# Layer 2's centring pass by 16 rows x 32 columns of all channels, with a second buffer for its stores

## The chip, the cores and the metric

The kernel runs on one core of a Trainium2 chip. The metric is device time in microseconds, from one launch to its end; the time before is the median of three runs. Durations, waits and packets come from one further execution that the hardware profiler recorded. The core's engines are PE (matrix multiply), DVE (vector), ACT (scalar, activations), POOL (GpSimd) and SP, which in this kernel issues every DMA; 16 DMA engines move the data.

## The reference

The input is 16 images of 64 x 64 tokens with 256 channels, fp32. Four layers follow one another, each `x = x + layer(group_norm(x))`:

```
x = x + _L0_conv_ref(_gn(x), ...)   # linear attention with a layer norm
x = x + _L1_conv_ref(_gn(x), ...)   # channel and spatial gates, a scan, batch norm
x = x + _L2_conv_ref(_gn(x), ...)   # 3x3 involution: kernels made from each token
x = x + _L3_conv_ref(_gn(x), ...)   # 7x7 involution, the same with 49 taps
```

What matters here is the input of the last layer. With `_gn` in 32 groups,

```
def _gn(v, G=32, eps=1e-5):
    g = v.reshape(B_, H_, W_, G, C_ // G)
    m = jnp.mean(g, axis=(1, 2, 4), keepdims=True)
    s = jnp.var(g, axis=(1, 2, 4), keepdims=True)
    return ((g - m) / jnp.sqrt(s + eps)).reshape(v.shape)
```

layer 3 needs each image minus its groups' means ("centred"), with a border of zeros, in 7 x 7 neighbourhoods: `out[h,w,c] = sum over 49 taps of kgen[h,w,group,tap] * centred[h+i-3, w+j-3, c]`. The division by the standard deviation is done elsewhere.

## The kernel before, in words

All instructions are unrolled; the kernel has three stages that follow one another. Stage a is layer 0 with the first statistics of layer 1, then comes a short stage for the scan and the statistics of layer 1 (until about 3,880 us), stage b does the end of layer 1 and all of layer 2, stage c is layer 3. Images pass between them through DRAM tensors: `x3_d` holds the output of layer 2, token after token with 256 channels (1 KB) each; `c3_d` holds the same with channels first; `strips` holds the centred image as layer 3 reads it: `strips[image, quarter, row, w, tile, 64]`. A quarter is 64 channels. A row is cut into NTC = 8 tiles of TC = 8 columns, and each tile is kept with three more columns on either side (w = 0 to 13), so a column near a tile's edge is stored twice. There are nine more rows and the outer columns that hold zeros. Stage c loads 128 consecutive (row, w) entries of it as 128 partitions of 2 KB.

Stage b (L912 to L1282) runs under a manual schedule, that is, instructions are issued in the order in which they are written. It runs 151 turns; in turn n, four lagged jobs each take one of eight parts (`rc`) of an image: `end_of_layer1` (lag 0: DVE multiplies, L989, ACT applies the gate, L995, POOL adds the input, L999; x2 is stored), `projected` (lag 12, PE, L1052), layer 2's involution (lag 20: PE transposes shifted rows, ACT copies them, L1102, DVE multiplies with the token's kernels, L1121, POOL sums the first half over nine taps, L1136 and L1137, DVE reduces the second half, L1271, and adds the residual, L1274), and `centred` (lag 30: the centring pass, for all images but the last). Statistics of the image that ended are made by `norm2` and `norm3` in between; `norm3` leaves the 256 means of an image on every partition (`gmb`).

The DMAs of a turn are all issued on SP's queue, in this order: loads for the next turn (x2p, x2r, x1 in two, pf in two), stores of what the turn before made (x2; x3 in two; c3 in two; 16 strip stores), and the load of the next turn's xc in two. A DMA takes one of eight completion semaphores in turn, and SP issues it only when the DMA before it on that semaphore has landed, so at most eight are under way.

The centring pass before: part `rc` of an image is one quarter of the channels in half of the rows. `centred_from` gives two sources in `x3_d`; `load_centred` (or the loop of stage c) loads them into `xc`, of 128 partitions x 16 rows x 64 channels: partition 64 g + w holds column w of 16 rows of image half g, and every run is 64 channels, 256 B. `centred_strips` subtracts the means in place (L892, POOL) and returns 16 stores: for either half g and each of eight tiles the 14 columns of the tile with its borders (11 at the image's edge) x 16 rows x 256 B. A tile `xc` has two buffers in stage b.

Stage c (L1286 to L1545) has 16 x 4 x 11 = 704 turns: one for each image, quarter and pair of tile rows. A turn loads patches for four turns ahead (`xw`, 6 buffers, L1414) and residuals (`rx`, L1434), runs 32 small matmuls against them (`involution7`, L1446), lets ACT, DVE and POOL combine two rows (L1456, L1457, L1464), makes part of the next quarter's matrices (`matrices`, L1380 to L1395), and stores. The centring of the last image is spread over this stage: at every 44th turn of the first eight images (n % 44 == 1) xc is loaded into one of the xw buffers (L1520), a turn later POOL subtracts, and of the 16 stores up to four are issued a turn (L1522).

`maps` and `fac` are small per-token maps of layer 1 (6.6 KB a partition) in the pool `gates`, which stays open until stage b ends.

Of the kernel before, what the change touches and what calls it, by code (L numbers as in the profile page):

```python
# [9 lines left out]
F32 = mybir.dt.float32  # L10
# [5 lines left out]
P = 128  # L16
C = 256
HW = 64
# [3 lines left out]
NB = 32  # L22
# [6 lines left out]
TR, TC = 3, 8  # L29
NTR, NTC = 22, HW // TC  # L30
# [6 lines left out]
def network(ctx: ExitStack, tc: tile.TileContext, a: dict, out: bass.AP):  # L37
    nc = tc.nc
    NI = a["x"].shape[0]
# [5 lines left out]
    def const(name, shape, src=None):  # L45
        t = cp.tile(shape, F32, tag=name, name=name)
        if src is not None:
            nc.sync.dma_start(out=t, in_=src)
        return t
# [5 lines left out]
    def gconst(name, shape):  # L55
        return gp.tile(shape, F32, tag=name, name=name)

    ident = const("ident", [P, P], a["ident"])
    gmat = gconst("gmat", [P, P])
    nc.sync.dma_start(out=gmat, in_=a["gmat"])  # L60
# [1 line left out]
    nc.vector.memset(mhalf, -0.5)  # L62

    ab = gconst("ab", [P, 2, NI, 2])
    fac = gconst("fac", [P, NI, NB])

    ngm1 = gconst("ngm1", [P, NI, 2])
    mean1 = gconst("mean1", [P, NI, 2])


    maps = gconst("maps", [P, 2, NI, NB + 4])
    nc.vector.memset(maps, 0.0)

    gm3 = const("gm3", [P, NI, 2])
# [7 lines left out]
    x3_d = dram.tile([NI, NT, C], F32, tag="x3_d", name="x3_d")  # L82
    c3_d = dram.tile([NI, P, 2, NT], F32, tag="c3_d", name="c3_d")
    strips = dram.tile([NI, 4, HW + 9, TC + 6, NTC, 64], F32, tag="strips", name="strips")
# [92 lines left out]
    with ExitStack() as st:  # L177
# [12 lines left out]
        for v in (wo[:, 0], wo[:, 1], bout):  # L190
            mean = small.tile([P, 1], F32, tag="wmean", name="wmean")
# [13 lines left out]
        wk = st.enter_context(tc.tile_pool(name="a_work", bufs=2))  # L205
# [5 lines left out]
        loaded, stores = {}, []  # L211

        def load(kind, i, ch):

            tag = {"xin": "xin", "xn": "xn"}.get(kind, "x1")
            t = wk.tile([P, 2, CT], F32, tag=tag, name=kind, bufs=4 if tag == "x1" else 2)
            src = a["x"][i, ch]
            if kind == "xm":
                src = x1_d[i, :, :, ch * CT : (ch + 1) * CT].rearrange("h p t -> p h t")
            nc.sync.dma_start(out=t, in_=src)  # L220
            loaded[kind, i, ch] = t
# [355 lines left out]
        for n in range(LAST + 16):  # L577
            m, t = divmod(n, NCH)
# [64 lines left out]
    with ExitStack() as st:  # L643
        pc = st.enter_context(tc.tile_pool(name="s_const", bufs=1))
        wk = st.enter_context(tc.tile_pool(name="s_work", bufs=3))
# [22 lines left out]
        with tc.tile_pool(name="s_conv", bufs=1) as pcv:  # L668
# [4 lines left out]
                out=lsa.rearrange("p i j c -> p (i j c)"), in_=a["lsa_w"].partition_broadcast(P)  # L673
# [27 lines left out]
        for n in range(10):  # L701
            delta, c = n // 2, n % 2
# [28 lines left out]
        with tc.manual_schedule():  # L731
            steps = [(ch, g) for ch in range(NCH) for g in range(NG)]
            rows, ins, hsts = {}, {}, {}
# [23 lines left out]
            for n, (ch, g) in enumerate(steps):  # L757
# [18 lines left out]
                b, k = g * 8, min(8, NI - g * 8)  # L776
# [8 lines left out]
        n = NI * NCH  # L785
# [61 lines left out]
            ALU.mult,  # L847
        )

    def folded(pool, name, mean, var, gamma, beta, shift):  # L850


        v = pool.tile([P, 5], F32, tag=f"{name}_v", name="v")
        for n, src in enumerate((mean, var, gamma, beta, shift)):
            if src is None:
                nc.vector.memset(v[:, n : n + 1], 0.0)
            else:
                for k in range(2):
                    nc.sync.dma_start(out=v[k * 64 : k * 64 + 64, n : n + 1], in_=a[src])
        sb = pool.tile([P, 3], F32, tag=f"{name}_sb", name="sb")  # L860
        nc.vector.tensor_scalar(v[:, 1:2], v[:, 1:2], BN_EPS, None, ALU.add)
        nc.gpsimd.tensor_tensor(v[:, 1:2], v[:, 1:2], mhalf[:, 0:1], ALU.pow)
        nc.vector.tensor_tensor(sb[:, 0:1], v[:, 1:2], v[:, 2:3], ALU.mult)
        nc.vector.tensor_tensor(v[:, 0:1], v[:, 4:5], v[:, 0:1], ALU.subtract)
        nc.vector.tensor_tensor(v[:, 0:1], v[:, 0:1], sb[:, 0:1], ALU.mult)
        nc.vector.tensor_tensor(sb[:, 1:2], v[:, 0:1], v[:, 3:4], ALU.add)
        nc.vector.tensor_scalar(sb[:, 2:3], sb[:, 0:1], -1.0, None, ALU.mult)
        return sb
# [11 lines left out]

    def centred_from(i, rc):

        quarter, q = divmod(rc, 2)
        x3n = x3_d[i].rearrange("(g r w) c -> g w r c", g=2, w=HW)
        return [
            x3n[g][:, q * 16 : q * 16 + 16, quarter * 64 : quarter * 64 + 64] for g in range(2)
        ]

    def centred_strips(i, rc, xc, mean):

        quarter, q = divmod(rc, 2)
        nc.gpsimd.tensor_tensor(  # L892
            xc, xc,
            mean[:, quarter * 64 : quarter * 64 + 64].unsqueeze(1).broadcast_to([P, 16, 64]),
            ALU.subtract,
        )
        parts = []
        for g in range(2):
            r0 = 3 + 32 * g + 16 * q
            for tj in range(NTC):  # L900
                lo, hi = max(0, tj * TC - 3), min(HW, tj * TC + TC + 3)
                c0 = lo - tj * TC + 3
                parts.append((
                    strips[i, quarter, r0 : r0 + 16, c0 : c0 + hi - lo, tj, :].rearrange(
                        "r w c -> w r c"
                    ),
                    xc[g * HW + lo : g * HW + hi],
                ))
        return parts


    with ExitStack() as st:  # L912
# [7 lines left out]
        gmb = {}  # L920
# [28 lines left out]
        loaded, stores, begun = [], [], []  # L949
# [8 lines left out]
        def taken(name):  # L958

            n = [k for k, _ in loaded].index(name)  # L960
            return loaded.pop(n)[1]
# [9 lines left out]
            ))  # L971

        def load_centred(i, rc):
            load("xc", [P, 16, 64], *(
                (lambda t, g=g: t[g * HW : (g + 1) * HW], src)
                for g, src in enumerate(centred_from(i, rc))
            ))

        def end_of_layer1(i, rc):
# [206 lines left out]
            )  # L1186

        def centred(i, rc):
            stores.extend(centred_strips(i, rc, taken("xc"), gmb[i]))

# [93 lines left out]
    with ExitStack() as st:  # L1286
# [201 lines left out]
        for n, (i, quarter, t) in enumerate(turns):  # L1488
            if quarter == t == 0:

                pm = sm.tile([P, CT], F32, tag="sm", name="pm")
                for k in range(2):
                    for j in range(2):
                        nc.tensor.matmul(
                            pm[64 * k : 64 * k + 64, 2 * j : 2 * j + 2],
                            lhsT=ident[:, 64 * j : 64 * j + 64], rhs=rs3[:, i, :],
                            start=True, stop=True,
                        )
                msk = small.tile([P, 2, 2, 2], F32, tag="msk", name="msk")
                nc.vector.tensor_tensor(  # L1500
                    msk.rearrange("p j k g -> p (j k) g"),
                    pm[:, 0:4].unsqueeze(2).broadcast_to([P, 4, 2]),
                    gpar.unsqueeze(1).broadcast_to([P, 4, 2]),
                    ALU.mult,
                )
            if t == 0:
                making = iter(())
                if n + NTT < len(turns):
                    making = matrices(*turns[n + NTT][:2])
            if n + 4 < len(turns):  # L1510
                pats.append(load_patches(*turns[n + 4]))
            if t % 2 == 0:
                ex = wk.tile([P, 2, TR * HW], F32, tag="ex", name="ex", bufs=4)
                rx = res.pop(0)
            if n + 2 < len(turns) and turns[n + 2][2] % 2 == 0:
                res.append(load_residual(*turns[n + 2]))
            if n % gap == 1 and n // gap < NCH:
                xc = wk.tile([P, 16, 64], F32, tag="xw", name="xc", bufs=6)
                for g, src in enumerate(centred_from(NI - 1, n // gap)):
                    nc.sync.dma_start(out=xc[g * HW : (g + 1) * HW], in_=src)  # L1520
            for dst, src in strip_stores[:4]:
                nc.sync.dma_start(out=dst, in_=src)  # L1522
            del strip_stores[:4]
            if done and done[0][0] == n:
                for dst, src in done.pop(0)[1]:
                    nc.sync.dma_start(out=dst, in_=src)  # L1526
            if n + 2 in features:
                cs[features[n + 2]] = load_reduced(*features[n + 2])
            involution7(i, quarter, t, wms[i, quarter], msk, pats.pop(0), ex[:, t % 2], rx[:, t % 2])
            if n % gap == 2 and n // gap < NCH:  # L1530
                strip_stores.extend(centred_strips(NI - 1, n // gap, xc, mean))
            for _ in range(STEPS[t]):
                next(making, None)
            if n in features:
                tp, k = features[n]
                reduced(k, tp, cs.pop((tp, k)))
            if t == NTT - 1:
                next(making, None)
                del wms[i, quarter]
            if t % 2 or t == NTT - 1:  # L1540
                parts = halves(ex, out[i, quarter * 64 : quarter * 64 + 64], t - t % 2)
                done.append((n + 3, [(d, s) for s, d in parts]))
# [111 lines left out]
```

## Time and profile before

| | us |
|---|---|
| Median of three runs | 8,946.06 |
| The runs | 8,943.62 to 8,962.98 |
| The profiled execution | 8,976.86 |
| Its span, first to last instruction | 8,974.9 |

Busy time in that span: PE 7,219.9 us (80%), weight loads 5,328.9 (59%), DVE 6,420.8 (72%), ACT 4,992.0 (56%), POOL 2,764.1 (31%); the DMA queue that SP feeds kept the 16 engines busy 62.5% of the time, with 1,616,994 packets of 1,682 MB. These shares are averages over stages of different kinds, so they don't say what sets the time in any of them; the tables by stretch do.

What the centring pass does in the profile: POOL's subtract L892 takes 2.36 us (120 times in stage b, 8 times in stage c at 2.38 us). There are 256 loads of xc, 256 KB each, and 2,048 strip stores, 1,536 of 56 KB and 512 of 44 KB. In stage b they run from 4,046 to 6,571 us, in stage c from 6,632 to 7,728 us.

Of the views: in a list of waits, "A <- B: total, times, longest" says that the engine of A stood idle before line A until B came. In a timeline a row has the start in us, the length, engine, line and operation, what is written from what, and how many were merged. A DMA row on SP is its issue, not its transfer.

### The profile page before, as it was taken

How to read it: one execution, taken by the hardware profiler on the slowest of the kernel's cores; microseconds unless marked ns; L12 is line 12 of the kernel's file. 1: busy time of each engine (PE TensorE's matmuls, PEld its weight loads, DVE VectorE, ACT ScalarE, POOL GpSimd, SP SyncE). 2: the span in 40 equal slices, each digit the busy share in tenths (PEclk: the TensorE clock that was granted, in tenths of full speed). 3: DMA queues.
4: the chain of work that ended last, by engine and by line, in shares of the span. 5: the costliest groups of instructions: out<-in, count | busy, mean ns of one | idle time of the engine just before them, and what ended most of it. 6: DMA issues, size and time to landing. Idle time of an engine off the chain costs nothing. (4 is left out here: it accounts for less than half of the span.)

```text
span 8974.9 us, 210876 instructions
## 1 busy us (share of the span) xinstructions
PE 7219.9 (80%) x84764; PEld 5328.9 (59%) x84764; DVE 6420.8 (72%) x8639; ACT 4992.0 (56%) x11904; POOL 2764.1 (31%) x1962
## 2 busy tenths in 40 slices
PE   7998988888899977477777777777758888888887
PEld 4666666666666653145554445545547666677776
DVE  6676666776666665679989988999946565566665
ACT  3555555555555554666655556565545555566655
POOL 0111111111111110157766666676712121111112
PEclk9999999999999987789888888888879999999999
DMA  6533333333333333867878878887768888888887
GB/s 219 167 121 122 122 124 123 125 118 125 127 106 104 106 113 118 250 201 219 222 215 226 223 217 223 227 224 211 182 193 240 248 249 244 247 256 255 255 256 233
DMA packets 1617971, 1695.46 MB, mean 189 GB/s; under 512 B 855265, under 2 KB 1221170, under 8 KB 1615842
## 3 DMA queue, kind: packets, MB, share of 16 engines
q1 hardware_dynamic: 1616994, 1681.98, 62.5%
q8 instruction: 668, 10.94, 0.5%
q14 instruction: 309, 2.53, 0.1%
HBM read 1234.54 MB, written 469.76 MB: 190 GB/s over the span
## 5 line engine op out<-in xcount | busy, mean ns | idle before, releaser
L279 PE MATMUL pq<-wq,xn 128*128 128x384 f32 x4096 | 1476.1, 504 | 105.4 <-DVE va L295 55.3
L1121 DVE TENSOR_TENSOR pd<-xs,pw 128x1152 f32<-128x1152 f32 x1024 | 1305.6, 1349 | 13.3 <-ACT xs L1102 13.3
L1380 PE MATMUL pk<-rt,span 64*128 64x176 f32 x12288 | 1217.4, 334 | 108.5 <-issue 58.5
L1395 DVE TENSOR_TENSOR wm<-pk,spanb 128x704 f32<-128x704 f32 x896 | 1174.2, 1354 | 171.6 <-PE pk L1380 157.7
L1390 ACT ACTIVATE wm<-pk,spanb 128x176 f32<-128x176 f32 x2560 | 989.8, 543 | 542.0 <-PE pk L1380 519.5
L1380 PEld LDWEIGHTS pk<-rt,span 64*128 64x128 f32 x12288 | 997.5, 195 | 212.5 <-issue 82.9
L1136 POOL TENSOR_TENSOR pd<-pd 128x2048 f32<-128x2048 f32 (+2 forms) x384 | 1064.6, 2772 | 180.9 <-DVE pd L1121 160.8
L279 PEld LDWEIGHTS pq<-wq,xn 128*128 128x128 f32 x4096 | 763.7, 195 | 572.7 <-DVE va L295 88.5
L1464 POOL TENSOR_TENSOR ex<-ex,rx 128x192 f32<-128x192 f32 (+2 forms) x768 | 436.8, 570 | 1888.1 <-DVE ex L1457 1401.0
L1446 PE MATMUL pa<-wm,xw 126*32 126x48 f32 x45056 | 694.4, 211 | 260.9 <-issue 245.8
L1457 DVE SCALAR_TENSOR_TENSOR ex<-pa,msk,ex 128x192 f32<-128x192 f32 x704 | 292.3, 415 | 752.2 <-ACT ex L1456 718.6
L1446 PEld LDWEIGHTS pa<-wm,xw 126*32 126x32 f32 x45056 | 574.4, 112 | 426.9 <-issue 376.2
L1098 PEld LDWEIGHTS pt<-ident,pad 128*128 128x128 f32 x4608 | 535.7, 150 | 239.6 <-issue 104.4
L1073 PE MATMUL pr<-x2r,wrs 128*64 128x512 f32 x512 | 364.5, 853 | 374.3 <-DMA x2r<-x_d 368.5
L1102 ACT COPY xs<-pt 128x512 f32<-128x512 f32 x1152 | 591.6, 602 | 121.1 <-PE pt L1098 115.5
L448 POOL TENSOR_TENSOR rsy<-ss,mhalf 128x4 f32<-128x4 f32 x128 | 129.8, 1014 | 1709.4 <-DVE ss L446 1709.4
L1098 PE MATMUL pt<-ident,pad 128*128 128x128 f32 x4608 | 615.7, 290 | 48.4 <-ACT rt L1076 29.3
L1271 DVE TENSOR_REDUCE x<-pd 128x512 f32<-128x4608 f32 x128 | 633.7, 4951 | 1.9
L1052 PE MATMUL px<-x2p,wis 128*128 128x512 f32 x1024 | 531.7, 664 | 111.4 <-ACT c L1150 68.2
L436 PE MATMUL py<-wo,oT 128*128 128x256 f32 x2048 | 472.8, 383 | 28.6 <-DVE va L295 28.6
L1456 ACT ACTIVATE ex<-pa,msk 128x192 f32<-128x192 f32 x704 | 298.3, 424 | 347.1 <-PE pa L1446 211.5
L445 ACT ACTIVATE sq<-y 128x256 f32<-128x256 f32 x512 | 213.0, 416 | 422.6 <-DVE y L441 414.6
(238 smaller groups left out, 12722.0 us busy)
## 6 DMA issues: line engine op xcount, KB each, us to landing
xw<-strips SPq DMA_DIRECT2D x1408, 256.0 KB
xn<-in_x SPq DMA_DIRECT2D x256, 512.0 KB
x_d<-x SPq DMA_DIRECT2D x256, 512.0 KB
strips<-xc SPq DMA_DIRECT2D x1536, 56.0 KB
xin<-in_x SPq DMA_DIRECT2D x128, 512.0 KB
x<-in_x SPq DMA_DIRECT2D x128, 512.0 KB
xm<-x_d SPq DMA_DIRECT2D x128, 512.0 KB
x<-x_d SPq DMA_DIRECT2D x128, 512.0 KB
```

What stands on the lines that cost most here:

```text
L279: nc.tensor.matmul(pq[:, dd, 0:384], lhsT=xn[:, h, tok], rhs=wq[:, h, hf * 384 : (hf + 1) * 384], start=(h == 0), stop=(h == 1),)
L436: nc.tensor.matmul(py[:, q, :], lhsT=oT[hf][:, q * P : (q + 1) * P], rhs=wo[:, hf, :], start=(hf == 0), stop=(hf == 1),)
L1052: nc.tensor.matmul(px, lhsT=w[:, h, fh * P : (fh + 1) * P], rhs=x2[:, h], start=(h == 0), stop=(h == 1),)
L1098: nc.tensor.transpose(pt[:, k, h * P : (h + 1) * P], lines[:, h, rc * 4 + e + k, 2 * j : 2 * j + P], ident,)
L1102: nc.scalar.copy(xs[:, e : e + 2, j, :], pt)
L1121: nc.vector.tensor_tensor(pd[:, r].rearrange("p (g f) k -> p g f k", f=16), run[:, oh * 9 * P : (oh + 1) * 9 * P].rearrange("p (g f k) -> ...
L1136: nc.gpsimd.tensor_tensor(pd[..., 0:n], pd[..., 0:n], pd[..., n : 2 * n], ALU.add)
L1271: nc.vector.tensor_reduce(x3[:, :, P:C], pd1, AX.X, ALU.add)
L1380: nc.tensor.matmul(pkv[:, b, m], lhsT=span[half, first + gg, s0 : s0 + P], rhs=rto[half, o // 4 * 2 + m, :], start=True, stop=True,)
L1390: nc.scalar.activation(dst[:, m // 2, m % 2], pkv[:, m // 2, m % 2], AF.Identity, bias=spanb[:, g0 + m : g0 + m + 1],)
L1395: nc.vector.tensor_tensor(dst, pkv, spanb[:, g0 : g0 + 4].rearrange("p (b m) -> p b m", b=2).unsqueeze(3).broadcast_to([P, 2, 2, NTL]), AL ...
L1446: nc.tensor.matmul(pav[p0 : p0 + 32, :, tj * TC : (tj + 1) * TC], lhsT=xw[0:TILE_IN, k, tj, 32 * q : 32 * q + 32], rhs=wm[q][0:TILE_IN, (t ...
```

## The change

A part of the image is now 16 rows x 32 columns of all 256 channels: `part` gives the rows, `th` the left or right half of the eight tiles. A partition holds tokens that lie 8 columns apart: partition 16 u + r has, for row r and column u within a tile, the four tiles of that half. The load is four DMAs, one a tile, in runs of 1 KB (256 channels). POOL subtracts the means from `xc` into a second tile, `cen`, in which the quarter comes before the tile, so that the four tiles of a quarter are 1 KB in a row, as they are in `strips`. The stores are twelve: for each quarter the 8 columns themselves, the last three columns as the right neighbours' left border, and the first three as the left neighbours' right border. In stage b `cen` has two buffers of its own; in stage c it takes another of the six buffers of `xw`. `maps` and `fac` move into a pool that is closed ahead of stage b.

```diff
+    maps_st = ExitStack()
+    mp = maps_st.enter_context(tc.tile_pool(name="maps", bufs=1))
...
-    fac = gconst("fac", [P, NI, NB])
+    fac = mp.tile([P, NI, NB], F32, tag="fac", name="fac")
...
-    maps = gconst("maps", [P, 2, NI, NB + 4])
+    maps = mp.tile([P, 2, NI, NB + 4], F32, tag="maps", name="maps")
...
+    maps_st.close()
...
     def centred_from(i, rc):
-        quarter, q = divmod(rc, 2)
-        x3n = x3_d[i].rearrange("(g r w) c -> g w r c", g=2, w=HW)
-        return [
-            x3n[g][:, q * 16 : q * 16 + 16, quarter * 64 : quarter * 64 + 64] for g in range(2)
-        ]
+        part, th = divmod(rc, 2)
+        x3n = x3_d[i].rearrange("(r t u) c -> u r t c", t=NTC, u=TC)
+        return [x3n[:, part * 16 : part * 16 + 16, th * 4 + t, :] for t in range(4)]

-    def centred_strips(i, rc, xc, mean):
-        quarter, q = divmod(rc, 2)
+    def centred_strips(i, rc, xc, cen, mean):
+        part, th = divmod(rc, 2)
         nc.gpsimd.tensor_tensor(
-            xc, xc,
-            mean[:, quarter * 64 : quarter * 64 + 64].unsqueeze(1).broadcast_to([P, 16, 64]),
+            cen.rearrange("p q t c -> p t q c"),
+            xc.rearrange("p t (q c) -> p t q c", q=4),
+            mean.rearrange("p (q c) -> p q c", q=4).unsqueeze(1).broadcast_to([P, 4, 4, 64]),
             ALU.subtract,
         )
         parts = []
-        for g in range(2):
-            r0 = 3 + 32 * g + 16 * q
-            for tj in range(NTC):
-                lo, hi = max(0, tj * TC - 3), min(HW, tj * TC + TC + 3)
-                c0 = lo - tj * TC + 3
+        rows = slice(3 + 16 * part, 19 + 16 * part)
+        for q in range(4):
+            for u0, u1, w0, dt in ((0, TC, 3, 0), (TC - 3, TC, 0, 1), (0, 3, TC + 3, -1)):
+                t0, t1 = max(0, th * 4 + dt), min(NTC, th * 4 + 4 + dt)
+                s0 = t0 - th * 4 - dt
                 parts.append((
-                    strips[i, quarter, r0 : r0 + 16, c0 : c0 + hi - lo, tj, :].rearrange(
-                        "r w c -> w r c"
-                    ),
-                    xc[g * HW + lo : g * HW + hi],
+                    strips[i, q, rows, w0 : w0 + u1 - u0, t0:t1, :].rearrange("r w t c -> w r (t c)"),
+                    cen[16 * u0 : 16 * u1, q, s0 : s0 + t1 - t0, :].rearrange("p t c -> p (t c)"),
                 ))
         return parts
...
         def load_centred(i, rc):
-            load("xc", [P, 16, 64], *(
-                (lambda t, g=g: t[g * HW : (g + 1) * HW], src)
-                for g, src in enumerate(centred_from(i, rc))
+            load("xc", [P, 4, C], *(
+                (lambda t, k=k: t[:, k], src) for k, src in enumerate(centred_from(i, rc))
             ))
...
         def centred(i, rc):
-            stores.extend(centred_strips(i, rc, taken("xc"), gmb[i]))
+            cen = wk.tile([P, 4, 4, 64], F32, tag="cen", name="cen")
+            stores.extend(centred_strips(i, rc, taken("xc"), cen, gmb[i]))
...
-                xc = wk.tile([P, 16, 64], F32, tag="xw", name="xc", bufs=6)
-                for g, src in enumerate(centred_from(NI - 1, n // gap)):
-                    nc.sync.dma_start(out=xc[g * HW : (g + 1) * HW], in_=src)
+                xc = wk.tile([P, 4, C], F32, tag="xw", name="xc", bufs=6)
+                for k, src in enumerate(centred_from(NI - 1, n // gap)):
+                    nc.sync.dma_start(out=xc[:, k], in_=src)
...
-                strip_stores.extend(centred_strips(NI - 1, n // gap, xc, mean))
+                cen = wk.tile([P, 4, 4, 64], F32, tag="xw", name="cen", bufs=6)
+                strip_stores.extend(centred_strips(NI - 1, n // gap, xc, cen, mean))
```

## The prediction

> **What bounds the kernel now.** I read the whole span first, then cut it by stage. Layer 2's pass runs from about 3,880 to 6,560 us, layer 3's from there to the end, and the change touches nothing before 3,880. So the next view is the busy time by stretch (columns: us, then busy time and instruction count of PE, weight loads, DVE, ACT, POOL; then granted clock, DMA share of the 16 engines, GB/s), for three stretches of layer 2's pass:
> ```profile
> 4225.00:4389.00 164.00, 123.06 (x660) 83.23 (x660) 156.49 (x130) 101.49 (x231) 119.91 (x59) 0.88 0.81 218
> 4472.00:6118.00 1646.00, 1192.66 (x6310) 812.54 (x6310) 1485.36 (x1230) 975.01 (x2189) 1131.97 (x552) 0.84 0.82 223
> 6118.00:6560.00 442.00, 304.43 (x1694) 211.93 (x1694) 385.29 (x308) 206.64 (x452) 295.74 (x128) 0.81 0.76 190
> ```
> The same view for the tensor_reduce of L1271, which runs once a turn, counts the turns:
> ```profile
> 4225.00:4389.00 164.00, 39.61 (x8) 0.88 0.81 218
> 4472.00:6118.00 1646.00, 376.18 (x76) 0.84 0.82 223
> ```
> So a turn takes 20.5 us in the first stretch, soon after centring has begun, and 1646/76 = 21.66 us in the long one. DVE is busy 95% there and 90% here: in the long stretch something else sets the pace. The waits of 4,472 to 6,118 us (us in total, times, longest) say what:
> ```profile
> PE pr L1073 <- DMA x2r<-x_d: 287.9, 55, 8.7
> DVE x L1274 <- POOL x L1137: 112.9, 60, 4.4
> DVE z L989 <- DMA pf<-fac_d: 27.8, 22, 4.5
> POOL x L999 <- DMA strips<-xc: 199.7, 31, 9.0
> SPq L955 <- DMA strips<-xc: 141.7, 161, 3.2
> ```
> PE waits for a load, POOL for a store, and DVE for POOL: transfers are late. Why, the order of SP's queue shows, over one turn:
> ```profile
> 5502.91 9.44 SPq L1228 DMA_DIRECT2D strips<-xc  x16
> 5514.40 1.33 SPq L955 DMA_DIRECT2D xc<-x_d  x2
> 5515.78 0.97 SPq L955 DMA_DIRECT2D x2p<-x_d  x1
> 5516.79 0.43 SPq L955 DMA_DIRECT2D x2r<-x_d  x1
> 5517.33 0.88 SPq L955 DMA_DIRECT2D x<-x_d  x2
> 5518.25 0.94 SPq L955 DMA_DIRECT2D pf<-fac_d  x2
> 5519.24 2.75 SPq L1228 DMA_DIRECT2D x_d<-x  x3
> 5522.74 1.31 SPq L1228 DMA_DIRECT2D c_d<-c  x2
> ```
> 29 DMAs follow one another with hardly a pause, each also waiting for the one eight before it (eight semaphores take turns). The one real pause is 5,512.35 to 5,514.40, 2.05 us: the load of the next xc goes into the buffer whose 16 stores were issued just before, and waits for all of them. In the packet records those stores move at 0.5 to 0.6 of the 16 engines, the engines then fall to nothing for 2 us, and from 5,516 to 5,528 all 16 are full. The DMA line of the stretch:
> ```profile
> DMA packets 610858, 366.34 MB, mean 223 GB/s; under 512 B 445361, under 2 KB 581553, under 8 KB 610744
> ```
> Three packets in four are under 512 B.
>
> [...] a store of 14 columns ends in 14 landings and one of 11 in 11[...], while the 64- and 128-partition transfers end in 16. [...] Here a 256 B packet has a median of 18 ns (14 GB/s), 1 KB 46 ns (22 GB/s), 4 KB 161 ns and, in layer 3, 768 B 36 ns. [...]
>
> **The change, part by part.**
>
> *The second buffer.* xc is now read by POOL alone, so its next load no longer waits for stores: the 2.05 us pause goes. The wait it adds is POOL's: the subtract of L892 must find the stores of two turns before landed. Behind it on POOL stands L999 of the next turn. Those stores are issued a whole SP cycle earlier and land some 5 us ahead by the order above, so I cost it at nothing; if the queue fell a further 5 us behind, it would show.
>
> *SP's queue.* 12 stores for 16 at about 0.46 us each with the gap (9.44 us has some lane waits in it): -1.85. Four loads for two, at about 0.65: +1.3. With the pause SP's cycle falls from 21.5 to about 18.9 us, so SP no longer sets it.
>
> *The engines.* [...] So the packets fall from 5,440 to 1,408 a turn[...].
>
> *The pace.* Compute alone needs 20.5 us a turn (the first stretch above, with the same POOL subtract and image boundaries in it); [...] I take 20.8 (my choice between 20.5 and 21.3). (21.66 - 20.8) x 76 = 65 us. Before 4,472 the pace is 20.5 and nothing is won. After 6,118 layer 1's loads are gone: [...] nothing is won or lost but the pause, up to -15.
>
> *POOL's subtract* keeps 1,024 elements a partition; it writes a permuted tile. Nearest rows: L892 at 2.36 us, L999 with a permuted output at 1.28 us per 512, so 2.36 to 2.56. POOL is busy 69% of the stretch; at most +15 us, taken as 0.
>
> *Layer 3.* Eight chunks of the last image run here, and cen takes one more of the six xw buffers. By the starts of L1456 an image of 44 turns takes 154.7 us with a chunk and 144.8 without one, so about 10 us hang on each chunk, SP's stores among the reasons. Four stores fewer and two loads more save 0.5 us of SP; [...] the next patch load waiting for POOL's subtract, cost something. Patches are fetched four turns ahead (13 us). Taken as 0, bounds -30 and +40.
>
> *maps and fac in a pool of their own* free their bytes for cen; no instruction is added. Nothing.
>
> Sum: -65 us. The profiled execution took 8,976.9 us (span 8,974.9), 30.8 above the median of the three runs; taken off the median, 8,946 - 65 = 8,881, say 8,880 us.
>
> **Rivals.**
> - *Compute alone bounds* (17%): [...] (packets overlap; the packet records show busy sums up to 1.4). Then 20.5 us a turn or, if POOL's wait at L999 goes too, DVE's 1485.36/76 = 19.5: -88 to -160 us, about 8,820. [...]
> - *No change* (10%): [...] a turn stays at 21.5 to 21.8; 8,935 to 8,960.
> - *Slower* (23%): [...] a turn is 23.0 us, over some 100 turns with centring +145 us, about 9,090. [...]
> - The forecast (50%): 8,880, its own range 8,850 to 8,920.
>
> **How the numbers follow.** The range 8,820 to 9,010 takes in the forecast, no change, most of the first rival and the lower half of the slower one. 0.2% (18 us) is about what this measurement can tell from no change. Faster 0.67 (50 + 17), same 0.10, slower 0.23.
>
> **What would show it.** Right: packets under 512 B nearly gone from 4,472 to 6,118; no SP pause ahead of xc; halo stores with 3 landings; L1271 at 20.5 to 21 us apart; DMA share falling to about 0.65 while lane waits stay on SP, now on strips<-cen. Wrong: turns of 22 us and more with growing waits for x2r and strips[...], POOL waiting at L892 for its stores, or layer 3 longer by over 40 us.

## The result, and the profile after

The changed kernel takes 8,805.49 us, the median of four runs (8,799.59 to 8,814.73), against 8,944.84 us (8,939.97 to 8,962.98) for the kernel before on the same chip: a ratio of 0.984, 95% interval 0.9828 to 0.9852. It is 139 us faster, where 65 were forecast, and below the low end of the range, 8,820. Two later comparisons on other chips gave 0.9831 [0.9813, 0.9848] and 0.9856 [0.9842, 0.9871]. The kernel before took 8,911 to 8,963 us from chip to chip, so what follows compares runs of one chip, or the length of a turn.

Line numbers have moved: POOL's subtract is L895, the stores are L1230, stage b's loads L957, DVE's reduce L1273 and its residual add L1276. First the busy time by stretch, as before (us, then busy time of PE, weight loads, DVE, ACT and POOL; then granted clock, DMA share, GB/s):

```profile
4225.00:4389.00 164.00, 122.84 (x660) 82.20 (x660) 157.02 (x132) 102.00 (x230) 120.88 (x59) 0.91 0.71 236
4472.00:6118.00 1646.00, 1236.92 (x6669) 849.39 (x6670) 1569.56 (x1302) 1011.75 (x2280) 1198.83 (x579) 0.88 0.70 233
6118.00:6560.00 442.00, 311.23 (x3148) 231.15 (x3146) 340.04 (x292) 211.64 (x499) 233.19 (x113) 0.81 0.58 185
```

In the long stretch DVE is now busy 1,569.56 of 1,646 us, 95%, where it was 90%, while the DMA share fell from 0.82 to 0.70. The waits of that stretch (us in total, times, longest):

```profile
ACT z L996 <- DVE z L990: 215.3, 57, 10.4
POOL x L1000 <- ACT z L996: 168.6, 44, 8.5
...
DVE x L1276 <- POOL x L1138: 62.6, 20, 5.7
...
POOL x L1000 <- DMA c_d<-c: 50.2, 8, 10.2
```

PE's 287.9 us for x2r and DVE's 27.8 us for pf are gone. Engines wait for engines. What is still put down to transfers is POOL's: 50.2 us "for c_d", 34.0 for x and 16.9 for x2r. The first deserve a second look. Here are two of its adds, 164 us apart, at the same place of two images that follow one another (in brackets the idle time ahead and what ended it):

```profile
5059.21 1.28 POOL L1000 TENSOR_TENSOR x<-z,x 128x512 f32<-128x512 f32 x1 [6.33 <-DMA c_d<-c]
...
5223.05 1.29 POOL L1000 TENSOR_TENSOR x<-z,x 128x512 f32<-128x512 f32 x1 [6.32 <-ACT z L996]
```

The idle time is the same to 0.01 us, once under a store's name and once under ACT's. A store that set it would hardly land on the same beat; most likely POOL waits for ACT both times, and the store merely came last by the records. The waits for x look alike: ahead of this add at 4,686.94 us POOL is idle for 2.40 us under x's name, and at the same place of the kernel without loads of xc (below) for 2.40 us under ACT's.

SP's queue over one turn and the start of the next:

```profile
5506.10 8.65 SPq L1230 DMA_DIRECT2D strips<-cen  x12
5514.79 2.50 SPq L957 DMA_DIRECT2D xc<-x_d  x4
5517.40 0.40 SPq L957 DMA_DIRECT2D x2p<-x_d  x1
5517.85 0.42 SPq L957 DMA_DIRECT2D x2r<-x_d  x1
5518.38 1.36 SPq L957 DMA_DIRECT2D x<-x_d  x2
5519.84 0.89 SPq L957 DMA_DIRECT2D pf<-fac_d  x2
5520.99 2.49 SPq L1230 DMA_DIRECT2D x_d<-x  x3
5524.22 1.08 SPq L1230 DMA_DIRECT2D c_d<-c  x2
5525.70 8.66 SPq L1230 DMA_DIRECT2D strips<-cen  x12
5534.40 2.85 SPq L957 DMA_DIRECT2D xc<-x_d  x4
5541.71 0.35 SPq L957 DMA_DIRECT2D x2p<-x_d  x1
```

The pause ahead of xc is 0.04 us, down from 2.05. SP's cycle is 5,534.40 - 5,514.79 = 19.6 us, and then SP stands from 5,537.25 to 5,541.71 for PE to free the buffer of x2p: here SP is ahead of the engines. The DMA line of the stretch:

```profile
DMA packets 306427, 384.10 MB, mean 233 GB/s; under 512 B 20967, under 2 KB 275588, under 8 KB 306308
```

Half the packets, and one in fifteen under 512 B instead of three in four.

Where the time went, from the starts of L1273 (one a turn) and of the first L1458, in us. "Again" are second profiles of either kernel:

| stretch | before | before again | after | after again |
|---|---|---|---|---|
| up to the first reduce | 3,886.8 | 3,878.5 | 3,875.5 | 3,884.8 |
| 29 turns | 585.1 | 584.9 | 575.1 | 574.6 |
| the next 76 turns | 1,646.5 | 1,644.6 | 1,560.5 | 1,560.5 |
| the last 22 turns, to layer 3 | 513.1 | 506.1 | 489.1 | 489.2 |
| layer 3 | 2,343.3 | 2,303.0 | 2,297.5 | 2,311.9 |

By the means of two, stage b gives 10.2 + 85.1 + 20.5 = 116 us. Layer 3 gives 18, but the two profiles of one kernel differ there by 14 and 40 us, so these four don't resolve it. A turn of the 76 went from 21.65 to 20.53 us.

### The profile page after: what moved, and what is told of

Same layout as the page of the kernel before. It is cut to its first block, busy times and chain, and to the rows that moved or that the text cites. A ratio compares the mean times of both kernels' runs of the same rounds, so it can differ in the third digit from the quotient of the medians.

```text
span 8797.7 us, 210558 instructions
## 1 busy us (share of the span) xinstructions
PE 7162.3 (81%) x84764; PEld 5301.9 (60%) x84764; DVE 6430.6 (73%) x8639; ACT 4982.1 (57%) x11904; POOL 2775.2 (32%) x1962
## 5 line engine op out<-in xcount | busy, mean ns | idle before, releaser
L1382 PE MATMUL pk<-rt,span 64*128 64x176 f32 x12288 | 1193.1, 331 | 55.9 <-issue 48.1
L1053 PE MATMUL px<-x2p,wis 128*128 128x512 f32 x1024 | 581.5, 715 | 199.2 <-ACT c L1151 131.9
L1099 PEld LDWEIGHTS pt<-ident,pad 128*128 128x128 f32 x4608 | 509.8, 145 | 278.4 <-ACT rt L1077 112.1
L1273 DVE TENSOR_REDUCE x<-pd 128x512 f32<-128x4608 f32 x128 | 633.4, 4948 | 1.9
L1053 PEld LDWEIGHTS px<-x2p,wis 128*128 128x128 f32 x1024 | 219.9, 229 | 459.3 <-issue 213.8
L1458 ACT ACTIVATE ex<-pa,msk 128x192 f32<-128x192 f32 x704 | 298.4, 424 | 327.7 <-PE pa L1448 168.6
```

The source lines that it names most:

```text
L1053: nc.tensor.matmul(px, lhsT=w[:, h, fh * P : (fh + 1) * P], rhs=x2[:, h], start=(h == 0), stop=(h == 1),)
L1099: nc.tensor.transpose(pt[:, k, h * P : (h + 1) * P], lines[:, h, rc * 4 + e + k, 2 * j : 2 * j + P], ident,)
L1273: nc.vector.tensor_reduce(x3[:, :, P:C], pd1, AX.X, ALU.add)
L1382: nc.tensor.matmul(pkv[:, b, m], lhsT=span[half, first + gg, s0 : s0 + P], rhs=rto[half, o // 4 * 2 + m, :], start=True, stop=True,)
```

## The experiments

**The kernel before, as a measure.**

> The kernel before once more, for a second profile of it. The profiled execution shown at first took 30.8 us more than the median of its kernel. If that lay in one stage, the split of the gain by stage has to be corrected: expected is a span near 8,945 us, turns of 21.6 us in 4,472 to 6,118 us again, and the 30 us missing from layer 3.

8,914.28 us, ratio 1.0 [0.9991, 1.0009]. So 0.1% can be told apart with ten runs beside fifteen; the kernels below had two to five runs, and intervals of 0.14 to 0.26% to either side. Of the 58 us by which this profile's span is shorter, 40 lie in layer 3, and a turn takes 21.64 us, much as expected.

**The second buffer alone.** The parts, loads and 16 stores of before; in stage b the subtract writes another tile. `maps` and `fac` are moved as in the change, to make room (not shown here); that move adds no instruction and was not run by itself.

```diff
-            xc, xc,
+            cen, xc,
...
-                    xc[g * HW + lo : g * HW + hi],
+                    cen[g * HW + lo : g * HW + hi],
...
+            cen = wk.tile([P, 16, 64], F32, tag="cen", name="cen")
...
```

> The old parts (256 B runs, 16 stores, 2 loads) with the second buffer alone, in layer 2's pass. Theory PACE (the queue's pause made the transfers late, and without it compute's own pace of 20.5 us a turn is all that is left): SP's cycle 21.6 - 2.05 = 19.6 us, below 20.5, so turns of 20.5 us and 8,945 - 105 = 8,840 us (8,815 to 8,865). Theory RUNS (the gain comes from fewer and longer packets): turns stay at 21.2 us or more, 8,900 us or more.

8,836.0 us, ratio 0.9909 [0.9895, 0.9924]; a turn takes 20.57 us. Busy time of the long stretch:

```profile
4472.00:6118.00 1646.00, 1259.63 (x6652) 868.12 (x6650) 1566.86 (x1301) 1015.80 (x2289) 1197.52 (x576) 0.86 0.86 233
```

With all the 256 B packets in place and the DMA engines busy at 0.86 rather than 0.70, DVE does as much as after the change (1,566.86 and 1,569.56 us). SP's waits ahead of the loads for stores of strips, 141.7 us in the stretch before, are gone: 1.4 us of them are left on the whole queue. The pace of the stretch comes from the second buffer: seven profiles of kernels with the changed stage b have turns of 20.53 to 20.74 us, and 20.57 lies among them.

The whole kernel is another matter. The second buffer alone gained 79 us on its chip; the changed kernel gained 130 to 145 on others, and the two were not run side by side. The rest has to be looked for outside the long stretch (below).

**The new parts with one buffer.** xc and cen are halves of one tile, so that the next load of xc again waits for the stores.

```diff
-            load("xc", [P, 4, C], *(
-                (lambda t, k=k: t[:, k], src) for k, src in enumerate(centred_from(i, rc))
+            load("xc", [P, 2, 4, C], *(
+                (lambda t, k=k: t[:, 0, k], src) for k, src in enumerate(centred_from(i, rc))
...
-            cen = wk.tile([P, 4, 4, 64], F32, tag="cen", name="cen")
+            xc = taken("xc")
+            cen = xc[:, 1].rearrange("p q (t c) -> p q t c", t=4)
...
```

> The new parts (1 KB runs, 12 stores, 4 loads), but in layer 2's pass xc and cen are two halves of one tile with two buffers, so that the next load waits for the stores again. PACE: SP's cycle of 19.9 us in the changed kernel plus a wait of 2 to 3.5 us for 12 stores, 22 to 23.4 us a turn, slower than the kernel before: 8,950 to 9,100 us. RUNS: 21 us a turn or less, 8,800 to 8,880 us.

9,150.96 us, ratio 1.0265 [1.0248, 1.0281]; a turn takes 23.75 us, more than expected. Its waits of the stretch, first the engines', then SP's:

```profile
PE pr L1074 <- DMA x2r<-x_d: 417.8, 60, 11.1
...
DVE x L1277 <- POOL x L1138: 187.8, 60, 4.5
...
DVE z L990 <- DMA pf<-fac_d: 114.8, 51, 6.1
```

```profile
SPq L957 <- DMA strips<-xc: 216.3, 178, 4.2
```

The pause ahead of xc in one of its turns:

```profile
5504.53 8.70 SPq L1231 DMA_DIRECT2D strips<-xc  x12
5516.56 2.54 SPq L957 DMA_DIRECT2D xc<-x_d  x4
```

The picture of before, worse. Where the stores' landing is waited for, the 1 KB layout costs 23.75 - 21.65 = 2.1 us a turn, and the pause is 3.33 us (5,513.23 to 5,516.56) where it was 2.05. It has half the packets, but a store ends in 8 or 3 landings (profile of after) instead of 14 or 11 (before), and in those two profiles the last landing comes 4.2 to 4.5 us after the issue instead of 2.4 to 2.5 (medians by shape in the stretch). Whether the number of landings is the reason was not separated from the other differences. With the second buffer nothing of it is left in the pace.

**The change in layer 2's pass alone, layer 3's last image centred as before.** Run on two chips, the second time beside the changed kernel.

```diff
-                xc = wk.tile([P, 4, C], F32, tag="xw", name="xc", bufs=6)
-                for k, src in enumerate(centred_from(NI - 1, n // gap)):
-                    nc.sync.dma_start(out=xc[:, k], in_=src)
+                xc = wk.tile([P, 16, 64], F32, tag="xw", name="xc", bufs=6)
+                for g, src in enumerate(old_from(NI - 1, n // gap)):
+                    nc.sync.dma_start(out=xc[g * HW : (g + 1) * HW], in_=src)
...
-                strip_stores.extend(centred_strips(NI - 1, n // gap, xc, cen, mean))
+                strip_stores.extend(old_strips(NI - 1, n // gap, xc, mean))
```

> The change in layer 2's pass alone; the last image is still centred in layer 3 by the old parts, in place. If layer 3's part of the change is worth the 46 us by which that stage is shorter in the second profile: 8,850 us. If that difference belongs to the first profile and not to the change (my theory): 8,800 to 8,820 us, as the changed kernel.

8,817.47 us, ratio 0.9892 [0.9874, 0.9911]. The time is what was expected of the changed kernel, but on this chip the kernel before took 8,915 us, 30 less than in the first comparison, and the ratio is worse than 0.984. Beside the second buffer alone, on the same chip and with the same layer 3, it is 19 us faster, with intervals that overlap.

> As the earlier run of it (the change in layer 2's pass alone; the last image centred in layer 3 by the old parts), now beside the changed kernel. No part of layer 3: the same time within 15 us. Layer 3 has a part: slower than the changed kernel by 20 to 45 us.

> The changed kernel once more, beside the next one on one chip, to size layer 3's part of the change. Its ratio to the kernel before was 0.984. If layer 3 has no part: the ratio of the next kernel lies within 0.2% of this one. In its profile a turn is 20.5 us.

On that chip 8,840.95 us, ratio 0.986 [0.9838, 0.9883], against 8,817.56 us, 0.9831 [0.9813, 0.9848], for the changed kernel: 23 us, with intervals that overlap a little. But 16 of the 39 us between the two profiles lie in the 76 turns of stage b (20.74 us a turn against 20.53), whose code is the same; the unchanged kernel itself took 20.64 in a third profile. All profiles together say a little more. Layer 3 takes 2,322.7 us on average in the five with the old parts in it (2,303 to 2,343) and 2,300.8 in the seven with the changed layer 3 (2,272 to 2,320; kernels that differ from after in stage b at most): 22 us, with a standard error of 11. So layer 3's part is probably worth some 20 us; the ranges overlap, and no run shows what would cause it.

**A store of 61 rows, and a control of 64.** One more store a turn, of cen's rows to a scratch tensor: 61 rows of 1 KB, or 64. In the records the semaphore packets of 4 B rise by about 1 a turn with 61 rows and by about 16 with 64; which engine carries a packet they don't say.

```diff
+            stores.append((scr[i, rc, 0:61, 0:256], cen[0:61, 0].rearrange("p t c -> p (t c)")))
```

> The changed kernel plus, in each of the 120 turns that centre, one store of 61 rows of 1 KB (of cen, into a scratch tensor)[...], SP one issue of about 0.7 us. [...] 23.2 us a turn, some +260 us. [...]

> Its control: the same extra store with 64 rows[...] and the same issue on SP. SP's cycle of 19.9 us becomes 20.6: a turn of 20.5 to 20.8 us, 0 to +30 us. [...]

With 61 rows: 9,031.43 us, ratio 1.007 [1.0044, 1.0096], a turn of 22.42 us. With 64 rows: 8,847.79 us, 0.9865 [0.9841, 0.989], 20.91 us. Both bring back the wait for x2r, first with 61 rows, then with 64:

```profile
PE pr L1075 <- DMA x2r<-x_d: 352.1, 61, 9.3
...
DVE x L1278 <- POOL x L1139: 155.5, 65, 4.3
```

```profile
PE pr L1075 <- DMA x2r<-x_d: 222.8, 51, 7.6
```

So about the same bytes cost 22.42 - 20.91 = 1.5 us a turn more as 61 rows than as 64. By the trace it is SP's queue that sets the turn there, which waits for the engines hardly at all (PE for 3.8 us in the stretch), but once a turn for the extra store itself to land, 106.0 us over 73 turns, or 1.45 us each:

```profile
SPq L958 <- DMA scr<-cen: 106.0, 73, 1.7
```

The 23.2 us expected rested on an estimate of the author's, that a DMA engine has no time left after the change; it is not shown. The control costs 0.38 us a turn for one more issue of 0.51 us and little data, and the wait for x2r is back with it, so SP has hardly any slack.

**No loads of xc.** POOL subtracts the means from a tile that is set once, so what is stored for the first 15 images isn't their centred tokens.

```diff
-            stores.extend(centred_strips(i, rc, taken("xc"), cen, gmb[i]))
+            stores.extend(centred_strips(i, rc, xc0, cen, gmb[i]))
...
-                if nxt_cen:
-                    load_centred(*nxt_cen)
```

> The changed kernel without the four loads of xc a turn in layer 2's pass: POOL subtracts the means from a tile that is set once to 0.5, so what is stored for the first 15 images is a constant minus the means and not their centred tokens; all stores, the subtract and layer 3 stay. It takes [...] some 2.5 us of issue from SP (cycle 19.9 to about 17.4 us). Theory COMPUTE ALONE: a turn of the stretch stays at 20.4 to 20.5 us, since transfers no longer set it; the time is within 30 us of after, DVE still waits for POOL and nothing else. Rival COUPLING[...]: the turn falls to 20.0 us or below, DVE's 19.5 being the least it can reach, and the time by 40 to 90 us.

8,755.91 us, ratio 0.9826 [0.9812, 0.9841]; a turn takes 20.16 us, between the two expectations. DVE, then SP:

```profile
DVE x L1276 <- POOL x L1140: 33.9, 12, 5.9
```

```profile
SPq L1232 <- POOL cen L895: 246.2, 82, 5.7
```

SP now waits in every turn for the subtract of that turn: transfers are ahead of the engines, and 20.16 us is what compute needs by itself in this profile. After the change DVE waits for POOL 20 times instead of 12, 62.6 us instead of 33.9, and over some 80 turns either way that is 0.36 of the remaining 0.37 us a turn. Whether SP's issue time or the transfers themselves cause it was not separated. Where in an image it lies, the starts of the reduce tell. Means over the 76 turns, in us, by the turn's place among the eight of an image:

| turn of the image | before | second buffer alone | after | no loads of xc |
|---|---|---|---|---|
| first | 23.72 | 24.70 | 24.56 | 23.63 |
| fourth | 21.50 | 22.59 | 22.43 | 20.20 |
| mean of the other six | 21.33 | 19.52 | 19.53 | 19.55 |

Six turns of eight run at the same pace in the three kernels without the pause, about the 19.5 us that DVE's own work takes. The first and the fourth turn of an image, its seams, are longer, and all that the loads of xc still cost is there. The pause cost in the six others.

**Layer 3: what a chunk still costs.** An image of 44 turns with a chunk of the last image takes about 150 us and one without about 140, in the kernel before as after. After the change TensorE (PE) stands in one such chunk for the next image's feature rows:

```profile
6684.65 1.55 PE L1349 MATMUL pr<-c,wr 128*64 128x192 f32 x8 [9.35 <-DMA c<-c_d]
```

Their load is issued on SP after the twelve stores and what queued up behind them. Two versions were tried beside the changed kernel: the load asked for four turns ahead, and that with two stores a turn instead of four.

```diff
-            for dst, src in strip_stores[:4]:
+            for dst, src in strip_stores[:2]:
...
-            if n + 2 in features:
-                cs[features[n + 2]] = load_reduced(*features[n + 2])
+            if n + 4 in features:
+                cs[features[n + 4]] = load_reduced(*features[n + 4])
```

> The changed kernel as it is, as the measure for the two that run beside it: ratio to before 0.983 to 0.985, some 8,805 to 8,820 us; a turn of layer 2's stretch 20.5 us; layer 3's turns with a chunk of the last image some 10 us a chunk longer than without.

> The changed kernel with layer 3's loads of the next image's feature rows asked for four turns ahead instead of two; all else as after. Theory LATE ROWS: what a chunk still costs in layer 3 is TensorE waiting for feature rows whose load stands on SP behind the chunk's twelve stores (9.35 us in one place of after's timeline); asked for four turns ahead, they are there. Each of the 8 chunks gives back 5 to 9 us: 40 to 70 us below after beside it, and TensorE's 9 us wait for the rows is gone. Rival SP'S OWN TIME: the 16 issues of a chunk hold SP for about 12 us, and whatever is behind them (patches, residual rows) is late next; then less than 15 us is won.

> As c3_four_ahead, and the chunk's twelve strip stores go out two a turn over six turns instead of four a turn over three. LATE ROWS: nothing more is won, within 10 us of c3_four_ahead. SP'S OWN TIME: spread over six turns the issues fit beside the turns' own loads and stores, and 20 to 50 us more are won. Against both stands that the centred tile holds one of the six patch buffers for three turns longer; if a patch load then waits for it, the time is 20 us or more above c3_four_ahead.

8,821.23 us (0.9856 [0.9842, 0.9871]), 8,814.81 (0.985 [0.9835, 0.9864]) and 8,817.47 (0.9853 [0.9837, 0.9869]): no difference that can be told. The first version fits SP'S OWN TIME, under 15 us, but the second won none of the 20 to 50 us that this theory promised it; LATE ROWS fails on the first. Nor is the second 20 us slower, as it would be if a patch buffer held longer had cost that much. The waits of 6,500 to 7,700 us, of after and then of the version with both edits:

```profile
PE pr L1349 <- DMA c<-c_d: 52.3, 8, 9.3
...
PE pa L1448 <- DMA xw<-strips: 18.4, 22, 2.8
```

```profile
PE pa L1448 <- DMA xw<-strips: 70.8, 81, 3.8
...
PE pr L1349 <- DMA c<-c_d: 0.4, 1, 0.4
```

The wait for the rows is gone, and 52 us more are spent in waits for patches; with the first edit alone the two waits are 15.0 and 45.4 us. By these single profiles the stall was moved, not removed. What a chunk's 10 us hang on stays open. No version was found that is faster than the changed kernel.

## Why the prediction was right or wrong

Right: faster, and the mechanism in stage b, a load of xc that stopped waiting for stores. The size was too small by more than half: 139 us against 65. Point by point:

- **The pause on SP** went, as said: 2.05 us to 0.04. The run with the second buffer alone shows that this is the whole gain of the long stretch (20.57 us a turn, 20.53 with the new parts).
- **SP's queue.** A store was priced at 0.46 us; twelve take 8.65 us, 0.72 each. The loads were right (2.50 / 4 = 0.63). The cycle came out at 19.6 us, not 18.9. It doesn't set the turn, but with 0.9 us to spare instead of the 1.9 that the forecast of 20.8 implied.
- **The engines.** A halo (a border store of three columns) ends in 3 landings, as said, and a main store in 8, by the packets of 4 B (the semaphore counts one more for either, 4 and 9). After's stretch has nearly the packet medians that were quoted (1 KB 46 ns, 768 B 36, 4 KB 159 where it was 161), but longer means: 50.4, 36.1 and 183.9 ns. That DMA engines would need about as long as compute was the author's estimate and was not shown, since the records don't tell which engine carries a packet.
- **The pace** is the step that failed: "Compute alone needs 20.5 us a turn (the first stretch above, with the same POOL subtract and image boundaries in it)". The stretch from 4,225 to 4,389 us is compute alone, since no engine waits for a transfer in it. But it is eight turns, one for each place in an image, with a first turn of 25.0 us, and the same eight take 20.4 us a turn after the change and without loads of xc too. Over 76 turns compute needs 20.16 (the kernel without loads of xc), with first turns of an image from 21.9 to 26.3 us. Moved by one turn, the eight take 20.85 before and 19.94 after. One image was too few for a pace to 0.3 us. With the loads 0.37 us are lost at the seams, about the 0.3 that I had added for coupling; that the sizes agree is luck, since I had put it down to DMA engines without time to spare, which was not shown. 20.16 + 0.37 = 20.53, where I had 20.5 + 0.3 = 20.8. That is 0.27 x 76 = 21 us of the miss.
- **After the long stretch** nothing was to be won "but the pause, up to -15", and the sum took nothing. The 22 turns with the passage to layer 3 gave 20 us, and the second buffer alone gives as much there (490.6 us against 513.1 and 506.1): it is the pause, and the term belonged in the sum.
- **Before the long stretch** nothing was to be won, and the 29 turns gave 10 us. This is not the pause, for the second buffer alone takes 586.1 us there, as before. Most of it is one turn at a seam, 27.6 us in both of these and 22.3 after. But the same turn of 27.6 us comes back later in some profiles of the changed stage b, and taken together the 29 and the 76 turns last 2,149 us with the second buffer alone and 2,135 to 2,150 with the new parts. What sets such a seam stays open. With the pace and the last turns that is 51 of the 74 us missed.
- **POOL's subtract** takes 2.37 us, against 2.36: nothing, as taken. **POOL's new wait** for the stores of two turns before does not appear among POOL's waits of the stretch.
- **Layer 3**, taken as 0 between -30 and +40, lies in the bounds. The remaining 23 us of the miss are probably here (18 us by the first profiles, 22 by all); the runs do not settle it.
- **The rivals.** "Compute alone bounds", at about 8,820 us, came nearest, though its 20.5 us was the true turn for another reason: compute is faster than that, and the seams cost the rest. The slower rival lost. The new parts do cost something where a landing is waited for, 2.1 us a turn in the kernel with one buffer, and the extra store 1.5 us more as 61 rows than as 64, but after the change nobody waits for the stores. That DMA engines decide between these rivals was the author's estimate and was not shown.
- **The signs.** The packets under 512 B, the pause, the halos' landings and the turn came as said; the DMA share fell to 0.70 and not to 0.65, and SP's waits for earlier DMAs are for loads (x2r 51.3 us, x2p 40.0), not for stores of cen.

## What to carry to other kernels

A pause on a queue that everything passes makes each load behind it late. Here 2.05 us in SP's queue cost 1.1 us a turn, all of it in six turns of eight; so give the buffer that stores hold a twin before reshaping the transfers, and try it alone. A pace called "compute alone" needs a stretch where nobody waits for a transfer, and one long enough: turns repeat with the image and its seams differ, so that eight turns gave 20.9 us before and 19.9 after, where 76 gave 21.7 and 20.5. Count turns between starts, and by their place in the image. Fewer, larger packets were no gain in the long stretch by themselves (20.53 us a turn against 20.57), and with one buffer they cost 2.1 us: look at whether anyone waits for their landing, and how long after the issue it comes.

## What the runs showed of the hardware

SP's time to issue a store goes with its shape, which I hadn't expected to matter so much. The first row is from the kernel before, the second from after (count, then min, median and max in ns):

```profile
L1228 SPq DMA_DIRECT2D strips<-xc x1920: 282/416/1975, 4088.3 to 6571.4; - x192
```

```profile
L1230 SPq DMA_DIRECT2D strips<-cen x1440: 628/683/1230, 4076.7 to 6433.8; - x180
```

Even the shortest store of the new kind takes 628 ns against 282. A store of 3 columns x 16 rows goes from 48 partitions, one of 14 columns from 14; the reason for the longer issue was not tested.

TensorE's granted clock in the stretch goes roughly with the pace: 0.81 at 23.75 us a turn (one buffer), 0.83 at 22.42 (61 rows), 0.84 at 21.65 (before), 0.85 at 20.91 (64 rows), 0.86 at 20.57 (second buffer), 0.88 at 20.53 (after), 0.90 at 20.16 (no loads). PE's busy time in the stretch is higher in the last of these than in the first, 1,250.62 us against 1,098.78 of 1,646, but the clock doesn't follow it throughout: with the second buffer PE is busy longest, 1,259.63 us, at 0.86. What sets the clock, and whether it gives something back, was not measured.
